# Expert tiles of 128 slots, two in a turn, and the attention residual by transposes

## The chip, the core and the metric

The kernel runs on one core of one Trainium2 chip. The metric is the device time of one execution, in microseconds (us). The kernel before takes 3216.83 us, the median of three runs (3212.77 to 3220.61).

A core has a matrix engine (TensorE, PE in the profile), a vector engine (VectorE, DVE), an activation engine (ScalarE, ACT), a general engine (GpSimd, POOL) and a sync engine (SP) that here issues nearly all transfers, one after the other, in program order. They run side by side and wait for each other by semaphores.

## The reference

The input is a batch of 8 images of 256 channels and 32x32 pixels, fp32. Two layers follow:

```python
x = x + conv_attn(group_norm(x), ...)     # layer 0, output projection w_out, b_out
t = tokens(x)                             # layer 1: 1024 tokens of 256 channels per image
t = t + attn(layer_norm(t), q_weight)     # sigmoid attention
t = t + moe(layer_norm(t), ...)           # 8 experts, the best 2 for each token
x = image(t)
```

Layer 0 samples 64 key positions per image at learned offsets and attends over them with a bias from a small three-layer network that is evaluated for every pair of pixel and key; that network is the largest part of the arithmetic. Its output projection is added to the layer's input.

The mixture of experts routes every token to its two best experts by a softmax over 8 logits:

```python
for e in range(8):
    h = gelu(tokens @ w1[e] + b1[e])      # 256 -> 256
    y = h @ w2[e] + b2[e]                 # 256 -> 256
    out = out + combine[:, e:e+1] * y     # combine is zero except for the token's two experts
```

## The kernel before

**The loop.** The eight images ("samples" 0 to 7) go through one loop of 8 x 64 turns. A turn n belongs to sample b = n // 64 and has the number i = n % 64 in it. Every turn does two pieces of the bias network of its sample: two `second_layer` calls, whose sixteen matmul instructions are line L466 and open the turn on TensorE, and in every second turn the third layer (L493). Everything else is hung onto the turns as generators that advance one step at a time: the preparation of the next sample (`prep`), the softmax of layer 0, the sigmoid attention of layer 1 (`attention`, in an upper half started at turn 53 and a lower half `rest` that runs in the next sample's turns from 0 on), the experts (`experts`) and the weighted sum of their outputs (`combine`). The instructions of each engine are tied to program order by `in_order`, so a step stands exactly where its turn put it.

**The residual.** In `to_query`, four matmuls per half and pair of token tiles put the layer's output projection into PSUM as tokens (L601: attention output `o` times `wo`, 256 columns). Then the layer's input `x`, which lies channels by pixels, is added in the same PSUM tile by multiplying it with the identity (L606, 128 columns). ScalarE copies the sum out (L610) as `x1`.

**Routing and sorting.** `route` finds the two best experts of each token and gives each token copy a row in a sorted array: the rows of an expert start at a multiple of `SLOTS` = 256, so that each tile of 256 rows belongs to one expert. 2048 copies and 8 experts need at most `TILES` = 15 tiles. `need` and `ends` count the tiles of each expert, `which` and `whose` name the expert of each tile, left as integers in `expert`. GpSimd scatters the rows to DRAM with sixteen indirect transfers (L763).

**The experts.** One step of `experts` is one round. Round n does three things for three tiles in a row, so that none waits for another: the second layer of tile n-2 (L896, result plus bias by VectorE at L901, stored at L904), the first layer of tile n-1 (L916, two GELUs at L922), and four transposes of tile n (L929, copied at L931). It also issues on the sync queue the fetch of the rows of tile n+2 (L874) and, after a register load of that tile's expert number (L878), both weight matrices of tile n+1 (L880, L882), into a pool `wpool` of three buffers each.

All 15 tiles are always run, also those that hold few or no rows. With two steps ahead and one behind, a sample's experts take 19 steps.

**When the steps fall.** `mix` has a hand-made table of due turns. Sample b's experts run during sample b+2, in turns 24, 26 and odd turns from 27 on without 35, 37, 39, 61 and 63, and their last three steps in turns 3, 7 and 9 of sample b+3. In sample 7 the experts of sample 5 run from turn 11 on, in odd turns and multiples of 6, up to turn 37; those of samples 6 and 7 run mostly after the loop, mixed with the last attention and routing (`while mains`) and then alone (`while mixtures`), beside the gathers of `combine` (L965).

## Time and profile before

| | us |
|---|---|
| time, median of three runs | 3216.83 |
| span of the profiled execution | 3216.8 |
| before the first turn | 73 |
| the eight samples' turns | 277.8, 337.3, 367.6, 376.0, 378.8, 375.1, 379.2, 393.8 |
| after the last turn | 258 |
| TensorE busy | 2928.8 (91%) |
| VectorE, ScalarE, GpSimd busy | 2173.7, 1841.1, 1547.5 |

Samples 0 and 1 carry no experts, which is why their turns are shorter. Busy time is the time in which at least one instruction of the engine was in flight; as matmuls overlap, the mean duration of a matmul (382 ns for L916) is longer than the distance from one to the next. A group of the profile reads: line, engine, operation, output <- inputs, shapes, count | busy us, mean ns of one | idle time of the engine just before, and whom it waited for. A row of the busy time by stretch reads: from:to in us, length, then for PE, PEld (weight loads), DVE, ACT and POOL the busy us and the number of instructions, then the granted TensorE clock, the share of the DMA engines and GB/s.

### The profile page before, as it was taken

The page shows a single profiled execution, that of the slowest core. Times are in us where ns is not written, and L with a number is a line of the kernel's source. Part 1 is how long each engine was busy: PE and PEld are TensorE (multiplying, and loading weights), DVE is VectorE, ACT ScalarE, POOL GpSimd, SP SyncE. Part 2 cuts the span into 40 slices and gives each one's busy share as a digit, 9 for nine tenths or more (in the row PEclk, how much of TensorE's full clock was granted, in tenths as well). Part 3 has the DMA queues.
Part 4 walks back from the last instruction along what each step waited for, and adds up shares of the span by engine and source line. Part 5 has one row for each costly group of instructions (what it writes and reads, how often), then busy time and mean ns, then how long its engine had stood idle before and what let it go on. Part 6 is the DMA issues. An engine that isn't in the chain of part 4 may idle for free. (4 is left out here: it accounts for less than half of the span.)

```text
span 3216.8 us, 50328 instructions
## 1 busy us (share of the span) xinstructions
PE 2928.8 (91%) x19468; PEld 1465.1 (46%) x19468; DVE 2173.7 (68%) x2996; ACT 1841.1 (57%) x2435; POOL 1547.5 (48%) x945
## 2 busy tenths in 40 slices
PE   3888998899999998999989999999999999988986
PEld 2223343334545454554535445354544546523765
DVE  4898678967785787756876587757777464586122
ACT  3666565656566556655566566655566566545322
POOL 2546344744464454634555365543646343364123
PEclk7999999999999999999999999999999999999998
DMA  3311101210344123432335224441234333532277
GB/s 100 89 32 45 21 19 27 69 29 19 85 122 129 32 65 98 136 91 50 87 88 145 55 61 103 117 133 33 66 90 141 81 84 97 147 96 64 66 248 235
DMA packets 421567, 281.20 MB, mean 87 GB/s; under 512 B 283088, under 2 KB 378064, under 8 KB 421328
## 3 DMA queue, kind: packets, MB, share of 16 engines
q1 hardware_dynamic: 408752, 242.80, 28.4%
q0 software_dynamic: 12288, 33.57, 3.4%
q8 instruction: 153, 2.51, 0.3%
q10 hardware_dynamic: 288, 1.62, 0.1%
q14 instruction: 86, 0.70, 0.1%
HBM read 204.51 MB, written 73.40 MB: 86 GB/s over the span
## 5 line engine op out<-in xcount | busy, mean ns | idle before, releaser
L453 POOL TENSOR_TENSOR h<-ta,nb 128x1024 f32<-128x1024 f32 x512 | 1060.7, 2073 | 1122.9 <-PE h2p L466 1052.8
L466 PE MATMUL h2p<-h,pr__97 64*64 64x512 f32 x8192 | 1026.8, 611 | 118.8 <-DVE h L474 86.8
L474 DVE TENSOR_TENSOR h<-h2p,nc 128x1024 f32<-128x1024 f32 x512 | 624.2, 1219 | 518.0 <-PE h2p L466 512.4
L472 ACT ACTIVATE h<-h2p,pr__97 128x1024 f32<-128x1024 f32 x512 | 569.7, 1113 | 516.0 <-PE h2p L466 514.9
L451 DVE TENSOR_TENSOR h<-ta,nb 128x1024 f32<-128x1024 f32 x512 | 765.3, 1495 | 0.7 <-ACT ta L427 0.5
L458 ACT ACTIVATE h<-h 128x1024 f32<-128x1024 f32 x512 | 536.8, 1049 | 82.8 <-POOL h L453 82.7
L466 PEld LDWEIGHTS h2p<-h,pr__97 64*64 64x64 f32 x8192 | 256.1, 133 | 639.9 <-issue 303.6
L493 PE MATMUL sim<-h,pr__97 128*32 128x512 f32 x4096 | 506.5, 613 | 0.0
L493 PEld LDWEIGHTS sim<-h,pr__97 128*32 128x32 f32 x4096 | 108.6, 111 | 375.4 <-issue 375.4
L896 PE MATMUL yp<-w,ht 128*128 128x256 f32 x960 | 241.8, 396 | 18.7 <-ACT tn L630 10.7
L701 PE MATMUL ap<-qt,tn 128*128 128x256 f32 x1024 | 250.5, 388 | 0.5 <-ACT nc L439 0.5
L715 PE MATMUL vp<-tt,sg 128*128 128x256 f32 x1024 | 243.3, 381 | 0.3 <-ACT sg L706 0.3
L922 ACT ACTIVATE ht<-hp,w 128x256 f32<-128x256 f32 x240 | 100.8, 471 | 239.9 <-PE hp L916 200.6
L916 PE MATMUL hp<-xg,w 128*128 128x256 f32 x960 | 229.4, 382 | 6.0 <-ACT gk L299 2.8
L965 POOL DMA_INDIRECT gs<-ys,slot x128 | 139.1, 1087 | 193.2 <-DMA ys<-yt 57.8
L701 PEld LDWEIGHTS ap<-qt,tn 128*128 128x128 f32 x1024 | 185.2, 190 | 88.5 <-issue 55.9
L896 PEld LDWEIGHTS yp<-w,ht 128*128 128x128 f32 x960 | 178.8, 195 | 85.1 <-issue 31.8
L715 PEld LDWEIGHTS vp<-tt,sg 128*128 128x128 f32 x1024 | 193.2, 190 | 33.2 <-issue 6.9
L901 DVE TENSOR_TENSOR yt<-yp,w 128x512 f32<-128x512 f32 x120 | 82.6, 688 | 176.6 <-PE yp L896 137.9
L916 PEld LDWEIGHTS hp<-xg,w 128*128 128x128 f32 x960 | 183.0, 191 | 33.3 <-ACT gk L299 3.7
L763 POOL DMA_INDIRECT xs<-ut,slot x128 | 166.9, 1304 | 47.9 <-DVE slot L850 26.2
L276 DVE SCALAR_TENSOR_TENSOR oc<-qp,pr__97,oc 128x128 f32<-128x128 f32 x280 | 168.7, 603 | 7.2
(264 smaller groups left out, 2550.6 us busy)
## 6 DMA issues: line engine op xcount, KB each, us to landing
w<-in_w SPq DMA_DIRECT2D x120, 384.0 KB, 3.9
ta<-fd SPq DMA_DIRECT2D x128, 256.0 KB, 5.5
w<-in_w SPq DMA_DIRECT2D x120, 257.0 KB, 3.2
xl<-xs SPq DMA_DIRECT2D x120, 256.0 KB, 3.0
ys<-yt SPq DMA_DIRECT2D x120, 256.0 KB, 2.3
nb<-fd SPq DMA_DIRECT2D x128, 128.0 KB, 5.2
xb<-in_x SPq DMA_DIRECT2D x8, 1024.0 KB, 7.9
x<-in_x SPq DMA_DIRECT2D x8, 1024.0 KB, 8.5
```

What stands on the lines that cost most here:

```text
L276: nc.vector.scalar_tensor_tensor(oc, tap, dw[:, t : t + 1], oc, ALU.mult, ALU.add)
L451: nc.vector.tensor_tensor(h1, a, b, ALU.max)
L453: nc.gpsimd.tensor_tensor(h1, a, b, ALU.subtract)
L458: nc.scalar.activation(h1, h1, AF.Relu)
L466: nc.tensor.matmul(h2p[gs, r, :], lhsT=par_("w2")[rs, gs], rhs=h1[rs, g].rearrange("p y x -> p (y x)"), start=True, stop=True, tile_positi ...
L472: nc.scalar.activation(h2, h2p, AF.Relu, bias=par_("cb2"))
L474: nc.vector.tensor_tensor(h2.rearrange("p r (y x) -> p r y x", x=W), h2p.rearrange("p r (y x) -> p r y x", x=W), nc_.unsqueeze(3).to_broad ...
L493: nc.tensor.matmul(sim[32 * q : 32 * q + 32, :], lhsT=par_("z3")[:, 15 - m : 47 - m], rhs=h2s[2 * u + q // 2][:, q % 2, :], start=False, s ...
L701: nc.tensor.matmul(ap[:, u, :], lhsT=tn[:, k, m0 : m0 + P], rhs=qt[:, k, quarter(q)], start=(k == 0), stop=(k == 1),)
L715: nc.tensor.matmul(vp[:, i, :], lhsT=sg_[:, u, i * P : (i + 1) * P], rhs=tt[:, 2 * mp + u, :], start=(first and u == 0 and i == 0), stop=( ...
L896: nc.tensor.matmul(yp[:, s, :], lhsT=ht[:, f, s * P : (s + 1) * P], rhs=f2[:, f * C : (f + 1) * C], start=(f == 0), stop=(f == 1),)
L916: nc.tensor.matmul(hp[:, f, :], lhsT=f1[:, k * C + f * P : k * C + (f + 1) * P], rhs=xg[:, k, :], start=(k == 0), stop=(k == 1),)
```

## The change

The tiles get 128 rows for all samples but the last, so that less of each is empty: at most 23 tiles, run as 12 rounds of two tiles each, where there were 15 of one. A round still moves 256 rows through the same steps, but it now holds the weights of two experts, in two pools of two buffers each; the first layer's weights are fetched later in the round and the second layer's one round later than before. The last sample keeps 256 rows and 15 rounds. In `mix`, three due turns go: 59, and 3 and 7 of the sample after.

The residual's products with the identity become transposes, which come first, and the output projection is added to them.

To make room for the weights, constants shrink to broadcasts and several small buffers are shared in `prep` and `route`.

```diff
-SLOTS = 256
-TILES = (2 * N + E * (SLOTS - 1)) // SLOTS
+LARGE, SMALL = 256, 128
+def tiles_of(slots):
+    return (2 * N + E * (slots - 1)) // slots
+TILES = tiles_of(SMALL) + 1
...
-    wpool = ctx.enter_context(tc.tile_pool(name="w", bufs=3))
+    w1pool = ctx.enter_context(tc.tile_pool(name="w1", bufs=2))
+    w2pool = ctx.enter_context(tc.tile_pool(name="w2", bufs=2))
...
-    ("ident", 128), ("gavg", 128), ("base", 512), ("basef", 128),
-    ("gq", 1), ("cx", 1), ("cy", 8), ("rev", 64),
-    ("ones", 128), ("before", 128), ("full", 256), ("tiles", (E - 1) * TILES), ("form", 12),
+    ("ident", 128), ("gavg", 128), ("base", 128), ("basef", 128),
+    ("gq", 1), ("cx", 1), ("cy", 8), ("rev", 8),
+    ("one", 1), ("before", 128), ("full", 8), ("upto", E * E), ("tiles", TILES), ("form", 12),
...
-        nc.scalar.activation(
-            oa.rearrange("p k (y x) -> p k y x", x=8), oc.rearrange("p (y k) x -> p k y x", k=2), AF.Gelu
-        )
+        nc.scalar.activation(oc, oc, AF.Gelu)
+        oa = oc.rearrange("p (y k) x -> p k y x", k=2)
...
                     for k in range(2):
                         nc.tensor.matmul(
-                            wp[:, u, :], lhsT=o[:, k, ts], rhs=wo[:, k, :],
+                            wp[:, u, k * P : (k + 1) * P], lhsT=x[:, k, ts], rhs=ident, is_transpose=True,
                             start=(u == 0 and k == 0), stop=False, skip_group_check=True,
                         )
                     for k in range(2):
                         nc.tensor.matmul(
-                            wp[:, u, k * P : (k + 1) * P], lhsT=x[:, k, ts], rhs=ident,
-                            start=False, stop=True, skip_group_check=True,
+                            wp[:, u, :], lhsT=o[:, k, ts], rhs=wo[:, k, :],
+                            start=False, stop=(k == 1), skip_group_check=True,
                         )
...
-            yield from route(lqs, rt)
+            yield from route(lqs, rt, LARGE if b == NB - 1 else SMALL)
...
-        nc.vector.tensor_reduce(ends[:, 1:9], need.rearrange("p e f n -> p e (f n)"), AX.X, ALU.add)
+        many = one.tile([P, E], F32, name="many")
+        nc.vector.tensor_reduce(many, need, AX.X, ALU.add)
+        nc.vector.tensor_tensor(
+            part(1), many.unsqueeze(1).to_broadcast([P, E, E]), cst_("upto").rearrange("p (e f) -> p e f", e=E), ALU.mult
+        )
+        nc.vector.tensor_reduce(ends[:, 1:9], part(1), AX.X, ALU.add)
...
+        slots_ = LARGE if b == NB - 1 else SMALL
+        several = LARGE // slots_
+        rounds = -(-tiles_of(slots_) // several)
...
+        def weights(t, pool, width, w, name):
+            f = pool.tile([P, 2, width], F32, name=name)
+            for u in range(several):
+                n = t * several + u
+                e = nc.sync.value_load(rt["expert"][0:1, n : n + 1], min_val=0, max_val=E - 1)
+                nc.sync.dma_start(out=f[:, u, :], in_=w[bass.ds(e, 1)].rearrange("e p c -> (e p) c"))
+            return f
...
-            if n + 2 < TILES:
+            if n + 2 < rounds:
                 fetch(n + 2)
-            if n + 1 < TILES:
-                weights(n + 1)
+            if n < rounds:
+                second[n] = weights(n, w2pool, 3 * C, w2_, "w2")
...
                 for f in range(2):
-                    for k in range(2):
-                        nc.tensor.matmul(
-                            hp[:, f, :], lhsT=f1[:, k * C + f * P : k * C + (f + 1) * P], rhs=xg[:, k, :],
-                            start=(k == 0), stop=(k == 1),
-                        )
+                    for u in range(several):
+                        us = slice(u * slots_, (u + 1) * slots_)
+                        for k in range(2):
+                            nc.tensor.matmul(
+                                hp[:, f, us], lhsT=f1[:, u, k * C + f * P : k * C + (f + 1) * P], rhs=xg[:, k, us],
+                                start=(k == 0), stop=(k == 1),
+                            )
...
-                for f in range(2):
-                    nc.scalar.activation(ht[:, f, :], hp[:, f, :], AF.Gelu, bias=f1[:, 2 * C + f : 2 * C + f + 1])
+                for f in range(2):
+                    for u in range(several):
+                        us = slice(u * slots_, (u + 1) * slots_)
+                        nc.scalar.activation(
+                            ht[:, f, us], hp[:, f, us], AF.Gelu, bias=f1[:, u, 2 * C + f : 2 * C + f + 1]
+                        )
+            if n + 1 < rounds:
+                first[n + 1] = weights(n + 1, w1pool, 2 * C + 2, w1, "w1")
...
-            due = i in (24, 26) or i > 26 and i % 2 and i not in (35, 37, 39, 61, 63)
+            due = i in (24, 26) or i > 26 and i % 2 and i not in (35, 37, 39, 59, 61, 63)
         elif of == b - 3:
-            due = i in (3, 7, 9)
+            due = i == 9
```

## The prediction

> **What bounds the kernel now.** First the page: busy time by engine and the forty slices.

> ```profile
> PE 2928.8 (91%) x19468; PEld 1465.1 (46%) x19468; DVE 2173.7 (68%) x2996; ACT 1841.1 (57%) x2435; POOL 1547.5 (48%) x945
> PE   3888998899999998999989999999999999988986
> ```

> TensorE is busy nearly throughout, so TensorE time taken away should count, but 9% is idle and has to be located. Second view, busy time by stage: the loop of samples 2 to 6, sample 7, the end up to the first transposes of sample 7's experts, those experts, and the last combine.

> ```profile
> core 0: us, PE busy (x) PEld busy (x) DVE busy (x) ACT busy (x) POOL busy (x), PEclk, DMA share, GB/s
> 688.10:2564.90 1876.80, 1788.39 (x12106) 899.72 (x12105) 1339.09 (x1846) 1141.51 (x1510) 952.78 (x569) 0.99 0.33 87
> 2564.90:2958.70 393.80, 361.21 (x2387) 179.50 (x2390) 252.12 (x322) 229.73 (x290) 188.43 (x125) 0.98 0.36 97
> 2958.70:3109.90 151.20, 136.89 (x652) 108.61 (x644) 35.13 (x101) 49.33 (x93) 25.34 (x30) 0.98 0.38 123
> 3109.90:3184.70 74.80, 67.28 (x313) 55.43 (x313) 15.16 (x28) 21.37 (x48) 15.47 (x16) 0.93 0.88 289
> 3184.70:3216.80 32.10, 6.21 (x21) 3.05 (x19) 9.23 (x19) 2.93 (x5) 15.43 (x16) 0.58 0.51 151
> ```

> The reader should see that TensorE fills 95% of the loop (1788 of 1877), that the last experts run with the DMA engines 88% busy, and that the final 32 us are a chain of gathers that the change doesn't touch. Third, the groups that the change touches:

> ```profile
> L896 PE MATMUL yp<-w,ht 128*128 128x256 f32 x960 | 241.8, 396 | 18.7 <-ACT tn L630 10.7 <-ACT ht L922 6.7 <-ACT nc L439 0.5
> L916 PE MATMUL hp<-xg,w 128*128 128x256 f32 x960 | 229.4, 382 | 6.0 <-ACT gk L299 2.8 <-DMA w<-in_w 1.2 <-PE yp L896 0.9
> L929 PE MATMUL tp<-cs,xl 128*128 128x128 f32 x480 | 73.9, 277 | 7.8 <-DMA xl<-xs 4.4 <-DVE yt L901 3.4
> ...
> L606 PE MATMUL wp<-cs,x 128*128 128x128 f32 x256 | 38.9, 274 | 0.0
> ```

> Durations overlap, so I price by the distance between starts in the timeline: 216 ns at 256 columns, 109 to 112 ns at 128, although the weights change every time (L606; L374 likewise). The counts add that a matmul of the code is two instructions (960 = 120 rounds x 4 x 2) while a transpose is one (480 = 120 x 4). So a round costs TensorE 8x216 + 8x216 + 4x109 = 3.89 us.

> Fourth, the turns (each begins with the first of sixteen L466 matmuls). Most repeat to a tenth of a us between samples, and samples 0 to 2 run some turns without the round that later ones carry there. Turns 59-60 of samples 1, 2 and 4, then turns 3-4 of samples 2 and 4:

> ```profile
> 658.51:671.46 12.95, 11.33 (x76) 4.03 (x72) 8.01 (x6) 10.10 (x15) 7.23 (x3) 1.00 0.16 32
> 1021.61:1039.08 17.47, 14.87 (x96) 7.40 (x92) 6.43 (x7) 10.12 (x17) 3.83 (x2) 1.00 0.44 138
> ...
> 1774.80:1793.94 19.14, 16.53 (x96) 8.62 (x92) 6.44 (x7) 10.12 (x17) 3.83 (x2) 0.91 0.48 143
> 705.39:717.73 12.34, 9.89 (x66) 2.51 (x62) 9.47 (x12) 6.35 (x8) 3.82 (x2) 0.86 0.01 1
> ...
> 1449.05:1462.49 13.44, 11.90 (x87) 5.81 (x83) 9.04 (x13) 8.95 (x12) 3.82 (x2) 1.00 0.06 21
> ```

> A round at turn 59 costs 4.5 to 6.2 us, more than its own work, because it also waits (L896 on the copies of L630). A round at turn 3 costs 1.1 us: without it TensorE merely waits for the softmax chain. So a removed round is not worth 3.89 us everywhere.

> Last, the sync queue in one round of the final stage:

> ```profile
> 3136.11 0.38 SPq L904 DMA_DIRECT2D ys<-yt  x1
> 3136.59 0.41 SPq L874 DMA_DIRECT2D xl<-xs  x1
> 3137.88 0.36 SPq L880 DMA_DIRECT2D w<-in_w  x1
> 3138.48 0.36 SPq L882 DMA_DIRECT2D w<-in_w  x1
> ```

> From the end of the row fetch to the end of the first weight transfer is 1.24 us, of which the register load of the expert's number is most; the second transfer adds 0.60. A round holds the queue for 2.73 us (3136.11 to 3138.84).

> [...] the trace has 216 ns for 256 fp32 columns,[...] and 109 to 112 for 128, so halving the columns halves the gap. [...] the trace has 362 for L439, 267 from start to start. [...] the instruction itself shows 270 to 470 here, and its register work follows.

> **The change part by part.**

> *Fewer rounds.* Seven samples go from 15 to 12 rounds of 256 rows, the last keeps 15: 99 instead of 120. By the due times the rounds lost are those at turn 59, and at 3 and 7 of the next sample.
> (a) Turns 59-60 of samples 2 to 6 take 17.5, 19.1, 19.1, 17.5, 19.2 = 92.4 us; without the round I take sample 1's 12.95: **-27.6**. Turn 57 loses its four transposes (0.44): **-2.2**.
> (b) Turns 3-4 and 7-8 of samples 3 to 6: 13.44 + 9.80 = 23.2 with rounds (sample 4), 12.34 + 10.29 = 22.6 without (sample 2): **-2.4** in all. The softmax chain and VectorE (9.35 of the 10.29 us) already set those turns.
> (c) Sample 7 carries sample 5's rounds in turns 11 to 37; they now end at turn 33. Its turns 31 to 38 take 49.6 us; without the rounds of 35 to 37, with lighter ones at 31 and 33 and the rest as in sample 2 (16.3 for 35 to 38) I get 37: **-12**.
> (d) At the end, sample 6's rounds run about one per 4.3 us until 3108.5, and sample 7's rows are fetched behind them at 3109.9. Three rounds fewer would be 13 us, but the scatters of L763 are issued until 3098.6 and take some 2.5 us to land, so the fetch comes at about 3101.4: **-8.5**.

> *Two experts in a round.* The first layer becomes 16 instructions of 128 columns instead of 8 of 256: 16x112 - 8x216 = 64 ns, in 84 rounds **+5.4**. The GELU becomes four of 128: 3x267 + 362 = 1.16 us against 0.84, +0.32 on ScalarE, 27 us in all; ScalarE is 61% busy in the loop, but turns such as 45 and 47 have it nearly full, so I charge **+5** (0 to 27).
> The weights: four register loads with transfers instead of one with two, 0.9 + 4x1.2 = 5.7 us on the sync queue a round. In the loop a round comes every 10 to 12 us and the transfers are used two rounds later: nothing, hidden by those turns. The first layer's reload now waits for the GELU of the same round; behind it on the queue stand the next result store and, at turn 56, the position terms (L423), which ScalarE wants (L427) some 16 us after that turn begins; with the queue held for about 3 us, four issues of 4 us and 5.5 us to land they need about 13. In sample 6's last rounds the queue (5.7) is slower than TensorE (4.3), but the scatters last as long; no charge beyond (d).
> Sample 7's rounds keep one expert, but the second layer's weights are issued in the round two before their use instead of three. Issued some 4.5 us into a round of 4.5 and landing in 4.9 (median in this stage), they are needed at 9.0: late by 0.4 per two rounds, 0.2 a round, **+3** (0 to 6).

> *The residual.* 16 half-samples, each with 8 products of two instructions (16x111 = 1.78 us), become 8 transposes (0.87): 0.9 each. Turns 5 and 54, where 15 of the 16 lie, have TensorE busy throughout (7.31 of 7.31, 9.17 of 9.17): **-14.5**.

> *Small things.* Routing gets one more small VectorE operation and slightly larger tables, about 0.15 us in a stretch where VectorE leads: **+1.2** over eight. The constants shrink from 1599 to 767 columns, 0.43 MB of the 2.9 MB that land before the first VectorE work at 9.80 us: **-1.3**. In-place buffers and the in-place GELU of the convolution cost nothing: the same operations on the same sizes, beside TensorE's work.

> Sum: -27.6 - 2.2 - 2.4 - 12 - 8.5 + 5.4 + 5 + 3 - 14.5 + 1.2 - 1.3 = -53.9, so **3163 us** from 3216.8.

> **The rivals.**
> *TensorE is the bound everywhere*: every removed round gives its 3.89 us, 21x3.89 = 81.7, with 14.5 of the residual less 5.4: 3126 us. For it: 95% busy in the loop. Against it: turns 3-4.
> *The removed work only uncovers waits*: as at turn 3 also at 59 and in sample 7, half of (a) and (c) is lost (20 us), ScalarE's 27 us count to the half (8 more): 3191 us. For it: turn 60 is slightly longer in sample 1 than in sample 4. Against it: 12.95 is a measured turn pair.
> *The sync queue becomes the bound*: where rounds stand close, 14 of sample 7's and 13 of sample 6's, the 3.0 us of added queue time lie on the path: +81, 3244 us, slower. For it: 5.7 exceeds 4.3. Against it: in sample 7's turns 11 to 33 a round has 6 to 12 us, and the last sample keeps single experts.

> **How the numbers follow.** My sum 0.60, TensorE everywhere 0.13, uncovered waits 0.17, sync queue 0.06, and 0.04 that all of it cancels. The sum's own unknowns (ScalarE 0 to 27, weights 0 to 6, turn 59 up to 7 us better) give 3148 to 3188; taking in the rival on each side nearly whole gives 3128 to 3194. Faster 0.91, same 0.03, slower 0.06.

> **What would show it.** L916 with 1464 instructions (84 rounds of 16, 15 of 8) some 112 ns apart in the pairs; L896 with 792; the residual with 128 transposes; turns 59-60 near 13 us; turns 3-4 and 7-8 hardly moved; sample 7's row fetch near 3050; its rounds at 4.5 to 4.7 us. I am wrong if L896 or L916 waits often on weight transfers, if h2p waits on ScalarE grow by more than 10 us, or if turns 59-60 keep 17 us.

## The result and the profile after

The changed kernel takes 3134.69 us, the median of four runs (3125.55 to 3140.18), against 3215.3 in the same comparison: 0.9744 of the time before, with a 95% interval of 0.9718 to 0.9771. That is 81 us less (74 to 91). A second comparison of the unaltered kernel gave 3132.65 us and 0.9754 (0.9740 to 0.9768). The forecast was 3163 us, 54 less: the side and the range were right, the size was a third too small.

The profiled execution of the change (span 3123.8 us) was the fastest of its four; a second trace of it has 3126.7. So the stretches below add up to 93 and 90 us, more than the 81 us of the medians. First the page's busy time and slices, then the stages as before: loop of samples 2 to 6, sample 7, the end up to the fetch of sample 7's rows, those experts.

```profile
PE 2832.1 (91%) x19592; PEld 1395.6 (45%) x19592; DVE 2170.5 (69%) x2999; ACT 1824.4 (58%) x2533; POOL 1558.2 (50%) x945
PE   3888998899999999999999999899999999979975
```

```profile
core 0: us, PE busy (x) PEld busy (x) DVE busy (x) ACT busy (x) POOL busy (x), PEclk, DMA share, GB/s
...
680.70:2492.13 1811.43, 1725.52 (x12243) 856.86 (x12242) 1337.91 (x1848) 1131.97 (x1586) 956.96 (x569) 0.99 0.38 103
2492.13:2867.12 374.99, 340.73 (x2374) 162.32 (x2374) 251.87 (x319) 222.97 (x297) 192.97 (x125) 0.98 0.42 114
2867.12:3013.50 146.38, 128.66 (x680) 103.13 (x672) 33.12 (x100) 49.06 (x108) 25.30 (x30) 0.95 0.48 154
3013.50:3091.97 78.47, 66.56 (x313) 54.34 (x313) 15.17 (x28) 21.29 (x48) 15.43 (x16) 0.96 0.85 275
```

TensorE is busy 97 us less and the span is 93 us shorter, so it is as full as before (91%); the slices of the loop, from the ninth to the thirty-second, still read 8 or 9. The loop of samples 2 to 6 gave 65.4 us (1876.8 to 1811.4) and sample 7 gave 18.8. The end gave almost nothing: the stretch up to the row fetch is 4.8 us shorter, the last experts 3.7 us longer. The groups confirm the counts:

```profile
L921 PE MATMUL yp<-w,ht 128*128 128x256 f32 x792 | 196.2, 390 | 13.7 <-DMA w<-in_w 7.0 <-ACT ht L947 5.4 <-ACT xg L959 1.0
L939 PE MATMUL hp<-xg,w 128*128 128x128 f32 x1344 | 166.7, 277 | 5.1 <-ACT gk L307 2.8 <-PE yp L921 0.9 <-DVE yt L926 0.8
...
L957 PE MATMUL tp<-cs,xl 128*128 128x128 f32 x396 | 60.8, 277 | 5.4 <-DMA xl<-xs 4.7 <-DVE yt L926 0.7
L939 PE MATMUL hp<-xg,w 128*128 128x256 f32 x120 | 30.3, 398 | 1.6 <-DMA w<-in_w 1.4
L613 PE MATMUL wp<-cs,x 128*128 128x128 f32 x128 | 25.5, 281 | 0.0
```

792 + 1344 + 120 instructions of the two layers belong to 99 rounds, and 128 transposes stand for the residual's 256. L921 now waits 7.0 us for weights (10.1 us in the second trace), which it did not before. The last view is that of the turns: 59-60 of samples 2 and 4, turns 3-4 and 7-8 of sample 4, turns 7-8 of sample 2.

```profile
1010.89:1022.33 11.44, 10.71 (x76) 3.95 (x72) 6.10 (x6) 8.60 (x14) 4.29 (x2) 1.00 0.27 77
1737.07:1748.51 11.44, 10.72 (x77) 3.95 (x73) 6.10 (x6) 8.60 (x14) 4.29 (x2) 1.00 0.27 71
1420.09:1430.79 10.70, 8.24 (x66) 2.33 (x62) 9.47 (x12) 6.35 (x8) 3.82 (x2) 1.00 0.01 2
1440.89:1449.52 8.63, 6.53 (x56) 1.94 (x52) 8.32 (x21) 4.12 (x4) 3.13 (x2) 1.00 0.01 2
718.68:728.98 10.30, 8.20 (x57) 2.12 (x53) 9.35 (x21) 4.12 (x4) 4.72 (x4) 0.83 0.00 0
```

Turns 59-60 take 11.44 us, not the 12.95 that I took from sample 1. Turns 3-4 take 10.70, not 12.34; turns 7-8 of sample 4 take 8.63, while those of sample 2, with the same work, take 10.30. The column that differs is the third from the right, the granted TensorE clock: 1.00 against 0.83. It stood at 0.86 in the row of sample 2 that the prediction quotes. The records of this trace and of that of before know only two clocks, full and half (1.0 and 0.5), and in the samples' turns the stretches at half clock come in pieces of 3.41 us, at times two or three in a row. Such a piece is called a half-rate window below.

By stretches, from the first trace of before to the two of after: turns 59-60 of samples 2 to 6 -35.2 and -35.2; turns 3, 4, 7, 8 of samples 3 to 7 -19.8 and -21.5; sample 7's turns 31 to 58 without 54 -10.6 and -10.6; turns 5 and 54 of all samples -15.1 and -13.2; then, the same in both, turn 57 of samples 2 to 6 -1.9, their odd turns 27 to 55, which keep a step of the experts, +5.7, turn 11 of samples 3 to 7 -6.4, and turns 35 to 40 of samples 2 to 6, which carry none, -5.0; samples 1 and 2 in turns 3-4 and 7-8 -4.8 and -3.4; the start -2.1 and -3.3; after the last turn -1.4 and -1.8. The rest sums to +3.6 and +6.4.

### The profile page after: what moved, and what is told of

It is laid out like the page before. It is cut to its first block, busy times and chain, and to the rows that moved or that the text cites. A ratio compares the mean times of both kernels' runs of the same rounds, so it can differ in the third digit from the quotient of the medians.

```text
span 3123.8 us, 51635 instructions
## 1 busy us (share of the span) xinstructions
PE 2832.1 (91%) x19592; PEld 1395.6 (45%) x19592; DVE 2170.5 (69%) x2999; ACT 1824.4 (58%) x2533; POOL 1558.2 (50%) x945
## 5 line engine op out<-in xcount | busy, mean ns | idle before, releaser
L465 POOL TENSOR_TENSOR h<-ta,nb 128x1024 f32<-128x1024 f32 x512 | 1071.6, 2095 | 1036.2 <-PE h2p L478 913.1
L478 PE MATMUL h2p<-h,pr__100 64*64 64x512 f32 x8192 | 1028.3, 610 | 131.8 <-DVE h L486 107.5
L947 ACT ACTIVATE ht<-hp,w 128x128 f32<-128x128 f32 (+1 forms) x366 | 108.6, 377 | 196.8 <-PE hp L939 173.2
L921 PE MATMUL yp<-w,ht 128*128 128x256 f32 x792 | 196.2, 390 | 13.7 <-DMA w<-in_w 7.0
L939 PE MATMUL hp<-xg,w 128*128 128x128 f32 (+1 forms) x1464 | 197.0, 287 | 6.7 <-ACT gk L307 2.8
L939 PEld LDWEIGHTS hp<-xg,w 128*128 128x128 f32 x1464 | 187.8, 194 | 18.3 <-ACT gk L307 3.7
L921 PEld LDWEIGHTS yp<-w,ht 128*128 128x128 f32 x792 | 144.4, 191 | 73.0 <-issue 34.0
L926 DVE TENSOR_TENSOR yt<-yp,w 128x512 f32<-128x512 f32 x99 | 68.3, 690 | 153.5 <-PE yp L921 127.3
```

Of the source, the lines that this page charges most:

```text
L465: nc.gpsimd.tensor_tensor(h1, a, b, ALU.subtract)
L478: nc.tensor.matmul(h2p[gs, r, :], lhsT=par_("w2")[rs, gs], rhs=h1[rs, g].rearrange("p y x -> p (y x)"), start=True, stop=True, tile_positi ...
L921: nc.tensor.matmul(yp[:, s, :], lhsT=ht[:, f, s * P : (s + 1) * P], rhs=f2[:, s * several // 2, f * C : (f + 1) * C], start=(f == 0), stop ...
L939: nc.tensor.matmul(hp[:, f, us], lhsT=f1[:, u, k * C + f * P : k * C + (f + 1) * P], rhs=xg[:, k, us], start=(k == 0), stop=(k == 1),)
```

## The experiments

All times are medians; "the change" is at 3132.7 us in the second comparison. The kernel before ran beside each of the three groups of runs and took 3213.8, 3216.1 and 3216.7 us there, so a difference of a few us between runs of different groups is not clear by itself.

**The change again, for a second trace.** No edit.

> The changed kernel, unaltered, for a second trace and a narrower interval. Theory A (half-rate windows of the TensorE clock fall by chance of phase): the stretches of a sample that carry no work of the change (turns 11, 36 to 40, 46, 52) differ from the first trace by 1 to 3 us wherever a half-rate window falls in one trace and not in the other, and the span lies 5 to 15 us above the first trace's 3123.8, since the other executions took 3133 to 3140. Theory B (the turns are fixed by the program): every turn repeats to 0.3 us and the span too.

Span 3126.7. Of 511 turns 482 repeat to 0.1 us; the other 29 move by up to 2.3 us. In both traces the eight samples contain 68 us at half clock, but not in the same places: turn 8 has a window in samples 2 and 3 of the first trace (7.9 us) and in sample 1 of the second; everywhere else in samples 1 to 6 it takes 6.3. All 29 turns lie in samples 0 to 3. From turn 10 of sample 3 on every turn repeats to 0.1 us, turns 11 and 36 to 40 too. So theory A holds at the beginning and theory B from there on, and the span is 3 us above the first, not 5 to 15.

**Identity products put back.**

```diff
-    wp[:, u, k * P : (k + 1) * P], lhsT=x[:, k, ts], rhs=ident, is_transpose=True, start=(u == 0 and k == 0), stop=False, ...
-    wp[:, u, :], lhsT=o[:, k, ts], rhs=wo[:, k, :], start=False, stop=(k == 1), ...
+    wp[:, u, :], lhsT=o[:, k, ts], rhs=wo[:, k, :], start=(u == 0 and k == 0), stop=False, ...
+    wp[:, u, k * P : (k + 1) * P], lhsT=x[:, k, ts], rhs=ident, start=False, stop=True, ...
```

> The change with the residual's identity products put back, nothing else. Price in the prediction: 16 half-samples of 0.9 us, so 14 us slower than the change (about 3149), with turns 5 and 54 each 0.9 us longer. Rival: the transposes also free something behind them (the copy of L610, the statistics), then 25 us or more and turns 6 and 55 move too.

3157.9 us, 25 more than the change, where 14 were priced. Yet turns 5 and 54 grew by 0.9 us each, exactly the price, and turns 6 and 55 didn't move, so the rival's reason isn't there. What moved is turn 8: 7.8 to 8.0 us in samples 1 to 6, in five of them with a half-rate window that the second trace of the change doesn't have there. The samples hold 85 us at half clock instead of 68. Two of these turns, of samples 3 and 4:

```profile
1094.85:1102.75 7.90, 5.93 (x34) 1.31 (x34) 7.06 (x14) 2.94 (x3) 3.59 (x4) 0.78 0.00 0
1460.50:1468.39 7.89, 5.91 (x34) 1.31 (x34) 7.07 (x14) 2.95 (x3) 3.58 (x4) 0.78 0.00 0
```

**The same, with turn 8 kept busy.** TensorE does more work, which nobody reads.

```diff
-        h2s += [second_layer(*h1s.pop(0)) for _ in range(2)]
+        for r in range(2):
+            h2s.append(second_layer(*h1s.pop(0)))
+            if r == 0 and b and i == 8:
+                fill()      # twelve nc.tensor.transpose(idle[...], ident, ident), idle = psum("idle")
```

> The run with the identity products, plus twelve transposes of a constant into an unread PSUM tile between the two second-layer calls of turn 8 in samples 1 to 7 (1.3 us, in a gap of some 2 us in which TensorE waits for VectorE). Its output is not touched by them. Theory clock (a half-rate window of TensorE falls into turn 8[...], and costs 1.6 us): turn 8 of samples 1 to 6 falls from 7.9 to about 6.3 us wherever the window stood, and the time falls by 5 to 10 us from 3157.9, although TensorE does more. Theory work (turn 8 is as long as its work and its waits): turn 8 keeps 7.9 us or grows by up to 1.3 us, and the time stays or grows.

3148.8 us, 9 less than without them. Turn 8 is 6.3 us in all of samples 1 to 6, at full clock:

```profile
1087.75:1094.00 6.25, 5.74 (x47) 2.42 (x47) 6.04 (x14) 2.95 (x3) 2.02 (x2) 1.00 0.00 0
1458.12:1464.37 6.25, 5.74 (x47) 2.42 (x47) 6.04 (x14) 2.95 (x3) 2.02 (x2) 1.00 0.01 3
```

Twelve more instructions (x47 against x34: the filler, and one record that the other trace lacks), 1.64 us less. Theory work is out. In sample 7, where turn 8 had no window (3.8 us), the filler costs 1.6 us.

**The change with the same filler.** Edit as above, on the change.

> The change plus the same twelve unread transposes in turn 8 of samples 1 to 7. Against the run with the identity products and these transposes (3148.8) it differs by the residual alone, with no half-rate window in turn 8 on either side. Theory clock (the 25 us between the change and the run with products were 14 us of work and the rest half-rate windows): 3130 to 3135, so 14 to 19 us under 3148.8, and turn 8 at 6.3 us in samples 1 to 6. Rival (the transposes free something else as well): 25 us under 3148.8, about 3124.

3133.2 us, 15.6 under the run with products and filler, inside what the clock theory gave. So the residual's transposes are worth 14 to 16 us (0.95 us in each of fifteen turns is 14.3), and most of the other 9 of the 25 were windows: the five more in turn 8 than in the second trace of the change, 1.6 us each, are 8. Against the change itself the filler brings nothing (3132.7): there turn 8 had one or two windows to lose, and sample 7 pays for the filler.

**Large tiles.** 256 rows and 15 rounds for all samples, the old due turns.

```diff
-            yield from route(lqs, rt, LARGE if b == NB - 1 else SMALL)
+            yield from route(lqs, rt, LARGE)
...
-        slots_ = LARGE if b == NB - 1 else SMALL
+        slots_ = LARGE
...
-            due = i in (24, 26) or i > 26 and i % 2 and i not in (35, 37, 39, 59, 61, 63)
+            due = i in (24, 26) or i > 26 and i % 2 and i not in (35, 37, 39, 61, 63)
-            due = i == 9
+            due = i in (3, 7, 9)
```

> The change with tiles of 256 rows for all samples, 15 rounds and the old due turns; transposes, smaller constants, weight pools and the order of the weight transfers stay. If the fewer rounds carry all but the residual and the start: 16 us faster than the kernel before, about 3199, and turns 3, 7 and 59 back at 7.7, 5.8 and 9.2 to 10.9 us. Rival (the later weight transfers or the pools themselves cost or gain): above 3210 or below 3190, to be seen in waits of L921 and L939 on the weights.

3204.8 us, 9 under before (ratio 0.9974, 0.9964 to 0.9983); its trace is 13 us under. Turns 3, 7 and 59 are back at their old lengths. The fewer rounds, with what two experts in a round cost, are thus worth 72 us of the change (3204.8 to 3132.7), windows included: this trace has 85 us at half clock in its samples, those of the change 68, those of before 81.6 and 71.4. The 7 us missing from the expected 16 are partly the end, 2.8 us longer than before, perhaps by the later weight transfers; the rest was not traced to a cause.

**Two more rounds, at turns 3 and 7.**

```diff
-TILES = tiles_of(SMALL) + 1
+TILES = tiles_of(SMALL) + 5
...
-        rounds = -(-tiles_of(slots_) // several)
+        rounds = -(-tiles_of(slots_) // several) + (2 if several > 1 else 0)
...
-            due = i == 9
+            due = i in (3, 7, 9)
```

> The change with two more rounds per sample (14 instead of 12, on rows that no token uses), at turns 3 and 7 of the next sample as before. Theory A (the prediction's step b: a round at 3 or 7 fills waits, 0.6 us for both): about 4 us in samples 3 to 7, and with two rounds each in sample 7's own turns and at the end about 20 us in all. Theory B (a round costs its 3.9 us of TensorE nearly everywhere, and the comparison of before was spoilt by half-rate clock windows in turns 4 and 8 of sample 2): turns 3-4 and 7-8 together about 4 us longer in each of samples 3 to 7, some 20 us there and 35 to 40 us in all.

3183.9 us, 51 more than the change. Turns 3-4 and 7-8 of sample 4 with these rounds:

```profile
1431.03:1444.49 13.46, 11.87 (x94) 6.09 (x90) 9.01 (x13) 9.18 (x14) 3.99 (x2) 1.00 0.25 79
1454.59:1464.45 9.86, 9.86 (x81) 5.36 (x77) 9.55 (x22) 5.23 (x8) 4.28 (x4) 1.00 0.09 28
```

Against the change's 10.70 and 8.63 that is 2.8 and 1.2 us, 4.0 for two rounds: theory B's figure for these turns, although a round is 3.9 us of TensorE. Half of it does fill waits, as I had said; I had said nearly all. The total is above theory B's 35 to 40. The remainder lies at the end (11.7 us for two rounds of sample 6, 5.8 each), in sample 7's turns (14.6, of which its own turns 3, 4, 7 and 8 are 5.9) and in turns 11 (10.0) and 36 to 41 (6.5), which carry nothing of the edit and hold more half-rate windows.

**One more round, at turn 59.** Likewise, with one more round and 59 put back into the due turns.

> The change with one more round per sample (13, the last on rows that no token uses), at turn 59 as before. Theory wait (a round there also waits in PSUM for the copies of L642, and its idle time brings a half-rate clock window): turn 59 goes from 2.9 to 9.2 to 10.9 us in samples 2 to 6, 32 to 40 us, with one round each in sample 7's turns (4) and at the end (6): 42 to 50 us slower than the change. Theory work (a round costs its 3.9 us): 20 us in samples 2 to 6 and 28 to 30 in all.

3164.5 us, 32 more. Turn 59 goes from 2.9 to 8.8 us (10.4 where a window fell), 31 us in samples 2 to 6. Theory wait is right on the mechanism and high on the total (42 to 50): only one of the five turns held a window, turn 60 gave back 0.25 us each time, and sample 7 cost only 2.6. The timeline of turn 59 of sample 4:

```profile
1753.96 1.09 PE L639 MATMUL bp<-cs,tt 128*128 128x128 f32 x8
...
1756.56 1.05 ACT L642 COPY tn<-bp 128x512 f32<-128x512 f32 x2
1757.19 1.59 PEld L921 LDWEIGHTS yp<-w,ht 128*128 128x128 f32 x8 [2.38 <-ACT tn L642]
1757.19 1.99 PE L921 MATMUL yp<-w,ht 128*128 128x256 f32 x8 [2.14 <-ACT tn L642]
```

Both transposed halves `bp` occupy the two PSUM buffers that `yp` shares with them; `yp` starts only when ScalarE has copied the first. A round here costs its 3.9 us and 2 us of that wait.

**The end: sample 6 with large tiles too.** `LARGE if b >= NB - 2 else SMALL` in both places.

> The change with 256 rows and 15 rounds for sample 6 as well. Theory queue: its rounds run every 4.3 to 4.7 us again, so three more of them cost 13 us and the relief of the queue gives back about 8 on the nine rounds after the attention; the fetch of sample 7's rows comes about 151 us after the last turn as in the kernel before (146 in the change), 3 to 6 us slower in all. Theory TensorE (the change's rounds of sample 6 are slow only because routing stands between them): rounds keep their spacing and three more cost 15 us or more.

3137.3 us, 4.6 more. This is not clear of noise: it is 0.9762 of the time before (0.9744 to 0.9779) where the change has 0.9754. Its trace is 11.2 us longer than the change's first, 8.4 of it after the last turn. The scatters start 4.7 us sooner after that turn (117.0 against 121.7) and the rows are fetched at 151.2 instead of 146.4. One round's sync queue, in the change and then here:

```profile
2989.90 0.38 SPq L927 DMA_DIRECT2D ys<-yt  x1
2990.33 0.46 SPq L900 DMA_DIRECT2D xl<-xs  x1
2992.03 4.39 SPq L907 DMA_DIRECT2D w<-in_w  x4
2996.53 0.38 SPq L927 DMA_DIRECT2D ys<-yt  x1
```

```profile
2985.19 0.38 SPq L927 DMA_DIRECT2D ys<-yt  x1
2985.62 0.47 SPq L900 DMA_DIRECT2D xl<-xs  x1
2987.68 1.55 SPq L907 DMA_DIRECT2D w<-in_w  x2
2990.89 0.38 SPq L927 DMA_DIRECT2D ys<-yt  x1
```

With two experts the next result store follows 0.1 us after the fourth weight transfer, although VectorE had its result ready 1.6 us before (at 2994.93), and the round takes 6.6 us: the queue is the pace. With one expert it takes 5.7, with 1.7 us to spare in the queue. From the first L921 of one round to that of the next, over sample 6's last rounds, it is 6.2 us in the change, 5.0 here, 4.9 in the kernel before. Theory queue holds for the pace of the rounds.

**The end: the second layer's weights from ScalarE's queue,** for samples 6 and 7.

```diff
-                e = nc.sync.value_load(...)
-                nc.sync.dma_start(...)
+                by = nc.scalar if name == "w2" and b >= NB - 2 else nc.sync
+                e = by.value_load(...)
+                by.dma_start(...)
```

> The change, with the second layer's weights of the last two samples loaded from ScalarE's queue instead of the sync queue. Theory queue (sample 6's last rounds are paced by 5.7 us of sync-queue work and sample 7's by the late second-layer weights): sample 6's last rounds fall from 5 to 8.5 us to about 4.5, the fetch of sample 7's rows comes 2 to 5 us sooner after the last turn, its fifteen rounds take 75 instead of 78.5 us, in all 4 to 8 us less than the change. Rival (the rounds wait for something else, or ScalarE's own order delays them): the end keeps its 256.6 us or grows, with waits of L940 or the GELU behind the loads.

3140.3 us, 8 more (0.9765 of the time before, 0.9752 to 0.9778), so not the 4 to 8 us less that were expected. The scatters start 6.2 us later than in the change. ScalarE in one round of sample 6:

```profile
2983.72 0.38 SPq L928 DMA_DIRECT2D ys<-yt  x1
2983.73 1.51 ACTq L908 DMA_DIRECT2D w<-in_w  x2
...
2985.28 1.14 ACT L948 ACTIVATE ht<-hp,w 128x128 f32<-128x128 f32 x4 [4.74 <-PE tp L958]
```

The transfers start when VectorE frees their buffer with `yt` (its end is at 2983.69 us), and the GELUs of the round stand behind them, from 2985.28 on. In all, L922's wait for the GELU's output is 11.3 us after the last turn, against 5.2 and 3.7 for the same in the two traces of the change, and its wait for weights (7.0 and 10.1 there) is gone: the rival named this delay. Sample 7's rounds, with one expert, did speed up as expected, to 64 us from the first L922 to the last against 67 for the same in the change. Together the time after the last turn grew by only 1.5 us. The loop before ran the same work and took 10 us longer than in the first trace of the change, 6 longer than in the second (81.6 us at half clock instead of 68), so a few us between two kernels can't be assigned to an edit without the trace.

**A round moved from turn 41 to turn 7.**

```diff
-            due = i in (24, 26) or i > 26 and i % 2 and i not in (35, 37, 39, 59, 61, 63)
+            due = i in (24, 26) or i > 26 and i % 2 and i not in (35, 37, 39, 41, 59, 61, 63)
-            due = i == 9
+            due = i in (7, 9)
```

> The change with one round moved in each of samples 2 to 6: out of turn 41, into turn 7 of the next sample. Theory fill (a round in turns 7-8 costs 1.2 us, as in the run with extra rounds there, because TensorE otherwise waits and falls to half rate; one in turns 40 to 53 costs about 2.2 us, as 83.8 against 68.2 us for seven of them in samples 4 and 1): 1 us less per sample and another 1.6 where a half-rate window stood in turn 8, so 5 to 10 us less than the change, 3123 to 3128. Rival (a round costs the same wherever TensorE is the bound): within 3 us of the change.

3137.5 us, 5 more, which is not clear of noise (0.9757 of the time before, 0.9741 to 0.9774), and not the 5 to 10 us less that were expected. The two places did what was priced: turns 7-8 of sample 4 grew by 1.2 us, and turns 40 to 53 shrank by 1.7 to 2.1 in samples 2, 3 and 5, which have no window there. But half-rate windows now fall into turn 11; its row here, and then in the change:

```profile
1463.13:1473.28 10.15, 7.28 (x26) 2.59 (x25) 5.84 (x5) 5.70 (x7) 9.77 (x6) 0.83 0.14 40
```

```profile
1458.31:1465.66 7.35, 5.57 (x25) 1.95 (x24) 5.67 (x5) 5.18 (x7) 6.97 (x6) 1.00 0.16 47
```

2.8 us from one window, three times the 0.9 that the move gains at most in a sample.

**The kernel before again.**

> The kernel before, unaltered, for a second trace. Theory clock: the half-rate windows stand in other turns or samples than in the first trace (there in turns 4 and 8 of samples 1 and 2, 11 of samples 4, 6 and 7, 59 of samples 3, 4 and 6), and each of these turns is 1.5 to 2.7 us shorter where the window is gone; the others repeat to 0.3 us. Rival: the same turns of the same samples again.

3217.9 us against 3216.7, no difference. Turn 4 of samples 1 and 2 is 6.9 us in this trace instead of 8.3 and 8.5, its windows gone; turn 11 has one in sample 3 and none in sample 4, the reverse of the first trace. Turns 8, 59, 11 of samples 6 and 7, and sample 7's later ones keep theirs. Both views were half right: the windows of turn 8 follow a wait of TensorE (1.97 us), which the program fixes, and whether one comes depends on something else.

The traces show what. Their records of the granted clock begin and end on a grid of 3.413 us, and the grid lies differently in each trace: its offset from the start of the span is 1.56 us in the first of this kernel, 0.60 in the second, 1.51 in the first of the change. Without a round and without the filler, turn 8 of samples 1 to 6 contains a wait of 1.97 or 1.98 us, here in sample 4 of the change:

```profile
1446.34 1.09 PE L478 MATMUL h2p<-h,pr__100 64*64 64x512 f32 x8 [1.97 <-DVE h L486]
```

Eleven traces contain 46 such waits. Of these, 21 lie whole between two lines of the grid, and a half-rate window follows each of them; 25 are cut by a line, and a window follows only 2, which are cut near their end. In the first trace of the change those of samples 2 and 3 lie whole: the waits end at 724.13 and 1082.47 us, the windows begin at 725.13 and 1083.53. The other four are cut, the one above by the line at 1445.35, and none is followed by a window. With the filler in it, 6 of 12 waits lie whole between two lines, and none is followed by a window.

No version tried beats the change.

## Why the prediction came out as it did

**Right: the view of the whole.** Fewer rounds on a TensorE that is 95% busy in the loop save time, but not 3.89 us each everywhere. Tile size with its due turns was worth 72 us for 21 rounds, 3.4 each on average. The rival with TensorE as the bound everywhere said 3126 us, nearer to the measured time than my 3163. Its sum fits the 72 us well (21 x 3.89 less the 10.4 priced for two experts in a round is 71.3), but a round does not cost the same everywhere: it cost 5.9 us at turn 59 (6.3 in the kernel before, where no window fell) and 2.0 on average at turns 3 and 7.

**Too small: step (b), turns 3-4 and 7-8.** Priced at -2.4 us for samples 3 to 6, measured there at -13.9 and -15.7 in the two traces. Sample 7, which the step left out although it had rounds at the same turns, gave 5.9 more. The mechanism was right in part (a round there fills waits: TensorE's waits for VectorE at the start of its second layer grew from 86.8 to 107.5 us in all); the comparison was wrong. I took sample 2's turns as the state without a round, and those contained two half-rate windows of the clock, 1.6 and 1.7 us, the first visible as 0.86 in the row that I quoted. The second is in turns 7-8, here of samples 2 and 4 of the kernel before:

```profile
728.78:739.07 10.29, 8.19 (x57) 2.16 (x53) 9.35 (x21) 4.12 (x4) 4.71 (x4) 0.83 0.01 2
1473.53:1483.33 9.80, 9.80 (x73) 4.92 (x69) 9.49 (x22) 4.96 (x6) 4.22 (x4) 1.00 0.09 29
```

Turns 3-4 and 7-8 without a window take 10.70 and 8.63 us, so two rounds cost 4.0 us, not 0.6. In turn 8 a wait of 1.97 us was enough for a window of 3.41 us at half clock, and with useless work in that wait none came (12 waits of the filler runs).

**Too small: step (a), turns 59-60.** -27.6 priced, -35.2 measured: 11.44 us in place of the 12.95 taken from sample 1. Sample 1 runs turns 55 and 57 without rounds and, as I read it, reaches turn 59 in another state: turn 58 takes 5.6 us there and 3.7 in a sample with rounds, and turn 59 without a round takes 4.1 us in samples 0, 1 and 7 and 2.9 in samples 2 to 6. Both figures contain the windows in turn 59 of samples 3, 4 and 6, 5.0 us together, which are gone with the round. A measured turn is a price only if the turns ahead of it are alike as well.

**Right: the residual.** -14.5 priced; turns 5 and 54 gave 0.9 us each, and the filler pair 15.6.

**Right in the sum, by luck: step (c), sample 7.** -12 priced for turns 31 to 38, -10.6 measured, but in turns 31 to 58. Turns 31 to 38 of sample 7, before and after:

```profile
2789.91:2839.53 49.62, 46.51 (x309) 23.42 (x308) 30.04 (x52) 28.40 (x40) 12.74 (x7) 0.97 0.40 108
2710.52:2753.59 43.07, 37.24 (x258) 13.55 (x257) 33.94 (x50) 24.54 (x35) 26.22 (x16) 0.88 0.45 104
```

They gave 6.6 us and not 12: turns 35 to 38 take 22.6 us and not sample 2's 16.3. The gathers of `combine` wait for the end of a sample's experts; those of sample 5 now fall into turns 34 to 48 instead of 39 to 53 (GpSimd 26.2 us busy against 12.7), and 10.2 us of turns 35 to 38 are at half clock. The prediction left both out. Turns 39 to 58, from which `combine` moved away, gave the other 4.0 us without a price.

**About right:** turn 57 (-2.2 priced, -1.9 measured), the start (-1.3, -2.1 and -3.3). The added cost of two experts in a round was priced at +10.4 for 84 rounds; the 60 rounds of samples 2 to 6 show +5.7, 0.1 us each, so the charge for ScalarE was a little high.

**Too large: step (d), the end.** -8.5 + 3 priced, -1.4 and -1.8 measured. Sample 7's rounds did slow by about the 3 us foreseen (3.7). But "the scatters last as long; no charge" failed: the sync queue paces sample 6's rounds at 6.2 us, routing stands between them, the scatters start 1.9 us later, the row fetch follows 5.6 us after the issue of the last one and not 3.8, and so it gains 4.8 instead of 8.5. In the second trace the fetch gains 7.1, and the time behind it is 5.3 longer. The rival with the sync queue was right about the pace of sample 6's rounds and wrong about sample 7's turns and about the total. The register loads of sample 7's rounds were misread too: in the kernel before they last 266 to 1048 ns, not 270 to 470, and 550 at the median of all 120.

**Missed: turns 11 and 35 to 40,** which carry no work of the change and gave 11 us in both traces. Turn 11's windows went; turns 35 to 40 shifted by one to two us with theirs. For a forecast this gain is luck: turns 11 of samples 3 to 7 take 38.3 us in both traces of the change, 44.7 and 44.6 in those of before, and anything from 37.2 to 48.3 in the other kernels above, whose turn 11 does the same work.

What stays open is how much of the 81 us is such chance. Before has 81.6 and 71.4 us at half clock in its samples, after 68 and 68; at half rate I estimate from these sums 2 to 7 us of lost TensorE time. The runs of one kernel spread over some 15 us (3125.6 to 3140.2 for the change, 3207.4 to 3224.9 for the kernel before), kernels with the same loop differ by 10 us in a trace, and the grid of the clock lay elsewhere in each trace (1.56 and 0.60 us from the start in those of before).

## What to carry to other kernels

Before a stretch is taken as the price of work removed, look at its granted clock and at what ran just ahead of it; turns 3-4 took 12.34 us at 0.86 and 10.70 at 1.00. Where the bound engine waits for a couple of us, some useful work put there may be half free, as it was here (4.0 us for two rounds of 3.9 each in turns 3-4 and 7-8), and may keep the clock up for what follows (turn 8: 7.90 us at 0.78, 6.25 at 1.00), but it has to be measured: the moved round lost elsewhere what it gained (3137.5 us against 3132.7). Work that is split finer is also issued more often (four transfers with register loads held the sync queue for 4.39 us, two for 1.55): count the issuing queue's time per round against the round's pace in the tightest stage, not in the average one.
